# Where a state-space scan starts its exponentials: before or after it waits for the scan ahead of it

## The chip, the cores and the metric

One core of one Trainium2 chip runs the whole program. The metric is the device time of one execution in microseconds, taken as the median of several runs. Engines are named as in the profile: PE (TensorE), DVE (VectorE), ACT (ScalarE), POOL (GpSimd), SP (the queue that issues most transfers). Each engine works through its own list of instructions in the order in which they stand there, and waits where an operand isn't there yet.

## The reference, cut to what matters

The program is two layers of a small perceiver over 16 sequences of 64 tokens with 256 channels (1024 tokens): cross attention, attention and a tiled feed-forward layer, then a second cross attention, a state-space layer, and a mixture of 64 experts. The change is in the state-space layer. Its core is a recurrence over the 64 tokens of a sequence, for 8 heads of 64 states:

```python
dt = jax.nn.softplus(dt_proj + dt_bias)
dA = jnp.exp(A[None, None] * dt[..., None])
dB = B_proj * dt[..., None]
def step(h, inp):
    dA_t, dB_t, C_t, x_t = inp
    h = dA_t[..., None] * h + dB_t[..., None] * x_t[:, :, None, :]
    y_t = jnp.einsum('bns,bnsd->bnd', C_t, h)
    return (h, y_t)
...
y_heads = y_heads + D[None, None, :, None] * x_heads
y = y_heads.reshape(B, L, d) * jax.nn.silu(z)
return y @ W_out.T
```

Its result is added to x, normalised, and routed to 8 of 64 experts for each token.

## The kernel before, in words

The 1024 tokens are 8 groups of 128 (two sequences each), g = 0 to 7. The recurrence isn't run step by step. For every pair of tokens of a sequence the decay between them is the exponential of A times a sum of dt over the tokens between. The pairs are split into 6 levels (NL), by the highest bit in which the two places differ; at each level the sum splits at a midpoint into a part of the earlier token and a part of the later one. So for each group there are 6 tables of sums of dt and a seventh that holds dt itself.

*What feeds the scans.* `inlet(g)` (line 271 on) makes the convolved input `xtok` and the raw `dtr` of a group. `sums(lo, hi)` (line 314 on) makes softplus of it for four groups, one matmul pair `ps_seg` (L351) makes all sums, ACT copies them to `sg`, and a transfer writes them to DRAM as `segd` (L353). `sw["summed"]` tells how many groups have their sums. `sums(0, 4)` is finished before the scans start, `sums(4, 8)` runs beside the first of them.

*A scan.* `scan(g)` works in these steps; the names are those of the profile.
- Two transfers on SP's queue read the sums back from `segd`, spread over 64 partitions each, into `e` (L1329, 2 x 896 KB, two buffers). Four ACT operations turn them into exponentials in place (L1335).
- PE makes `ps_B` (L1340), DVE multiplies it by dt to `bt` (L1342); PE makes `ps_C` (L1347), ACT copies it to `cT` (L1349); PE makes the gate `ps_z` (L1353), ACT takes its tanh `zt` (L1361).
- For each level DVE makes `pb` from `bt` and `e` (L1365) and POOL makes `pc` from `cT` and `e` (L1366). DVE completes `zt` (L1369), POOL makes `pd` (L1371).
- Three rounds of two levels each: PE makes `ps_g` (L1380, 32 matmuls a round, each two records in the profile for every matmul of the source), and DVE writes it into the 128 x 128 matrix `gt` by masked copies (L1390, four a round). After the first round `sw["half"]` is set to g + 1.
- The diagonal: `ps_dg` (L1401), `dg` (L1403, DVE), `yt` (L1405, POOL). Then `ps_y` = `gt` times `xtok` (L1410), two DVE operations `yt` (L1411, L1412), PE's transposes `ps_yT` (L1416), ACT's copy `yT` (L1418), the output product `ps_o` (L1423), and DVE's addition to x (L1424).
- `route(g)` follows: a layer norm (DVE, with `rs_mo` by POOL at L205 and its result `xtok` at L216), transposes `psx_mo` (L1183), logits (L1188), some forty small DVE operations that pick the experts, places `ps_pos` (L1236), and the slots `idx` (L1248). For each token eight POOL scatters `xbuf` (L1158) send its row to its experts' slots; `post(n)` issues them four at a time inside later scans. `shared()` does the shared expert beside it (`ps_se` L1439, `hT_s` L1443 and L1444, `ps_sy` L1448).

*The order.* `drive` (line 235 on) is a small planner that runs while the program is built. Each scan is a generator that issues some instructions and yields two numbers, a cost and a gap in assumed microseconds; `drive` takes whichever generator is due next. At most two scans are active; a scan that yields "tail" (after `ps_o`) no longer counts, and the next one starts. `until(test)` yields until the test holds. Below `drive`, the framework may still interleave neighbouring pieces on an engine. All of it is fixed when the program is built: the chip sees one list for each engine.

In the code before, a scan's first step is this, and the next yield stands behind the exponentials:

```python
yield from until(lambda: sw["summed"] > g and sw["half"] >= g)
...
yield 0, 12.0
```

Every PSUM tile of the program comes from one pool of 8 buffers that are handed out in order.

Of the kernel before, what the change touches and what calls it, by code (L numbers as in the profile page):

```python
# [147 lines left out]
def perceiver_kernel(ctx: ExitStack, tc: tile.TileContext, a: dict, consts: bass.AP, out: bass.AP):  # L148
# [115 lines left out]
    sw = {"done": 0, "routed": 0, "half": 0}  # L264
    segd = dram.tile([NG * NH, (NL + 1) * P], F32, name="segd")

    def until(test):
        while not test():
            yield 0, 0.5
# [1006 lines left out]
    with p2:  # L1276
# [43 lines left out]
        def scan(g):  # L1320
            pb, gt = pbs[g % 2], gts[g % 2]
            tk = slice(g * P, (g + 1) * P)

            yield from until(lambda: sw["summed"] > g and sw["half"] >= g)

            e = wrk.tile([P, 4, NL + 1, P], F32, tag="e", name=f"e_{g}")
            src = segd.rearrange("(g j q) k -> g q j k", j=4, q=2)
            for q in range(2):
                nc.sync.dma_start(  # L1329
                    out=e[q * 64 : (q + 1) * 64, :, :, :].rearrange("p j l k -> p j (l k)"),  # L1330
                    in_=src[g, q].partition_broadcast(64),
                )
            dts = e[:, :, NL, :]
            for j in range(4):
                A.activation(e[:, j, 0:NL, :], e[:, j, 0:NL, :], AF.Exp, scale=Ac[:, j : j + 1])  # L1335
            yield 0, 12.0
            pm = psm([P, 4, P], f"ps_B_{g}")
            for j in range(4):
                for c in range(2):
# [115 lines left out]
        def wtile2(shape, name):  # L1455
# [3 lines left out]
            (2, [maker(inlet, g, wide("xn"), wtile2) for g in range(NG - 2, NG)]),  # L1459
            (1, [maker(sums, 4, NG)]),  # L1460
            (2, [maker(scan, g) for g in range(NG)]),
            (1, [outward, shared]),
        )
# [153 lines left out]
    with tc.If(n > CAP):  # L1617
        with tc.For_i(0, E) as e:
# [9 lines left out]
            for q in range(4):  # L1628
# [12 lines left out]
                for i in range(2):  # L1641
                    g = 2 * q + i
# [36 lines left out]
```

## Time and profile before

| | us |
|---|---|
| median of 3 runs | 1093.58 (1093.21 to 1094.02) |
| the profiled execution: its own time | 1105.71 |
| its span | 1103.9 |
| PE busy (share of the span) | 900.0 (82%) |
| DVE busy | 612.9 (56%) |
| ACT busy | 269.0 (24%) |
| POOL busy | 274.3 (25%) |
| transfers of `e` issued, first and last | 608.3 and 780.3 |
| first `ps_B` to last `ps_o` | 619.4 to 855.6 |
| last scatter to the experts' slots issued | 886.4 |

The scans take the stretch from 608 to 856 us of the span; before it lie both cross attentions and layer 0, after it the experts. Times below are microseconds from the start of the span of the profiled execution, which as a whole took 12 us more than the median of the runs. The clock of PE that the profile lists is a share of full speed; over the whole execution it was 0.878.

### The profile page before, as it was taken

How to read it: one execution, taken by the hardware profiler on the slowest of the kernel's cores; microseconds unless marked ns; L12 is line 12 of the kernel's file. 1: busy time of each engine (PE TensorE's matmuls, PEld its weight loads, DVE VectorE, ACT ScalarE, POOL GpSimd, SP SyncE). 2: the span in 40 equal slices, each digit the busy share in tenths (PEclk: the TensorE clock that was granted, in tenths of full speed). 3: DMA queues.
4: the chain of work that ended last, by engine and by line, in shares of the span. 5: the costliest groups of instructions: out<-in, count | busy, mean ns of one | idle time of the engine just before them, and what ended most of it. 6: DMA issues, size and time to landing. Idle time of an engine off the chain costs nothing. (4 is left out here: it accounts for less than half of the span.)

```text
span 1103.9 us, 16706 instructions
## 1 busy us (share of the span) xinstructions
PE 900.0 (82%) x6242; PEld 685.4 (62%) x6242; DVE 612.9 (56%) x1903; ACT 269.0 (24%) x608; POOL 274.3 (25%) x326
## 2 busy tenths in 40 slices
PE   4978888978898888978885788889988369999945
PEld 3755565655665565655644567778877258778724
DVE  1446564556546654555557747657866863333316
ACT  0314132222224132222224422113210022232210
POOL 0000100001100100000102112555565525556540
PEclk7879999999999999999887757677786579999978
DMA  7511150310420150111301632444411958888236
GB/s 235 172 38 61 61 180 1 121 61 28 154 108 14 62 180 1 60 62 44 111 2 37 153 72 68 108 108 98 108 47 41 351 184 286 280 291 287 72 121 265
DMA packets 70712, 130.60 MB, mean 118 GB/s; under 512 B 10083, under 2 KB 56607, under 8 KB 67558
## 3 DMA queue, kind: packets, MB, share of 16 engines
q1 hardware_dynamic: 56016, 107.97, 30.3%
q0 software_dynamic: 7680, 17.33, 4.5%
q10 hardware_dynamic: 6934, 4.23, 1.4%
q8 instruction: 50, 0.82, 0.3%
q14 instruction: 32, 0.26, 0.1%
HBM read 97.54 MB, written 36.14 MB: 121 GB/s over the span
## 5 line engine op out<-in xcount | busy, mean ns | idle before, releaser
L1524 POOL DMA_INDIRECT ybuf<-yo,goal x96 | 93.5, 974 | 87.3 <-DVE yo L1551 28.8
L1516 PE MATMUL ps_ee<-xT,wq 128*128 128x192 f32 x512 | 95.4, 330 | 0.2 <-ACT xT L1506 0.2
L1516 PEld LDWEIGHTS ps_ee<-xT,wq 128*128 128x128 f32 x512 | 81.8, 190 | 6.7 <-issue 3.5
L1158 POOL DMA_INDIRECT xbuf<-xtok,idx x64 | 68.1, 1064 | 66.4 <-DVE idx L1248 41.1
L989 PE MATMUL fpy<-fw,fxm 128*128 128x256 f32 x256 | 59.3, 391 | 13.3 <-DVE fxm L986 6.8
L625 PE MATMUL po_a<-cn,paT_a 128*64 128x256 f32 (+1 forms) x416 | 54.3, 395 | 15.7 <-ACT paT_a L619 7.7
L989 PEld LDWEIGHTS fpy<-fw,fxm 128*128 128x128 f32 x256 | 49.5, 196 | 23.9 <-issue 16.0
L1380 PEld LDWEIGHTS ps_g<-pc,pb 64*128 64x128 f32 x768 | 56.9, 228 | 10.5 <-POOL pc L1366 4.9
L1380 PE MATMUL ps_g<-pc,pb 64*128 64x64 f32 x768 | 59.8, 316 | 2.7 <-DVE zt L1369 1.6
L625 PE MATMUL po_b<-cn,paT_b 128*64 128x256 f32 (+1 forms) x416 | 50.2, 385 | 9.2 <-DVE paT_b L619 8.3
L205 POOL TENSOR_TENSOR rs_ff<-ve_ff,neghalf 128x1 f32<-128x1 f32 x8 | 4.4, 548 | 204.8 <-DVE ve_ff L203 193.3
L399 PE MATMUL psc<-ct,cn 128*128 128x128 f32 x384 | 51.9, 287 | 2.6 <-DMA cn<-in_ctx_dram 2.5
L1390 DVE COPY_PREDICATED gt<-ct,ps_g 128x256 f32<-128x256 uint32 x96 | 43.2, 538 | 12.3 <-PE ps_g L1380 7.3
L399 PEld LDWEIGHTS psc<-ct,cn 128*128 128x128 f32 x384 | 46.5, 149 | 5.5 <-issue 3.3
L587 PE MATMUL sc_b<-cT,qT_b 128*64 128x512 f32 (+1 forms) x256 | 47.5, 525 | 2.1 <-DVE qT_b L559 1.6
L1366 POOL TENSOR_TENSOR pc<-cT,e 128x256 f32<-128x256 f32 x48 | 36.3, 790 | 46.6 <-ACT cT L1349 46.5
L625 PEld LDWEIGHTS po_a<-cn,paT_a 128*64 128x64 f32 (+1 forms) x416 | 27.3, 139 | 32.4 <-ACT paT_a L619 8.7
L1518 ACT ACTIVATE hg<-ps_ee 128x192 f32<-128x192 f32 x64 | 21.4, 334 | 106.6 <-PE ps_ee L1516 39.2
L1504 PE MATMUL ps_xT<-ct,xg 128*128 128x128 f32 x192 | 30.5, 287 | 19.5 <-DMA xg<-xbuf 19.5
L587 PE MATMUL sc_a<-cT,qT_a 128*64 128x512 f32 (+1 forms) x256 | 46.4, 505 | 0.0
L194 ACT COPY cT<-psc 128x512 f32<-128x512 f32 x51 | 29.8, 588 | 66.8 <-PE psc L399 66.2
L625 PEld LDWEIGHTS po_b<-cn,paT_b 128*64 128x64 f32 (+1 forms) x416 | 27.8, 136 | 25.3 <-DVE paT_b L619 10.0
(438 smaller groups left out, 1858.2 us busy)
## 6 DMA issues: line engine op xcount, KB each, us to landing
cn<-in_ctx_dram SPq DMA_DIRECT2D x16, 1536.0 KB
e<-segd SPq DMA_DIRECT2D x16, 896.0 KB
xbuf<-zero SPq DMA_DIRECT2D x8, 1632.0 KB
xg<-xbuf SPq DMA_DIRECT2D x16, 816.0 KB
wq<-in_L_ffn_We_gate_dram SPq DMA_DIRECT2D x16, 512.0 KB
wq<-in_L_ffn_We_up_dram SPq DMA_DIRECT2D x16, 512.0 KB
wq<-in_L_ffn_We_down_dram SPq DMA_DIRECT2D x16, 512.0 KB
yg<-ybuf SPq DMA_DIRECT2D x8, 1024.0 KB
```

Source lines behind the costliest of these rows:

```text
L194: A.copy(dst, src)
L399: T.transpose(ps[:, j, :], cn[:, 4 * q + j, c * P : (c + 1) * P], ident)
L587: T.matmul(sc[b * 64 : (b + 1) * 64, :], lhsT=qT[:, c, b * 64 : (b + 1) * 64], rhs=cTs[2 * g + b][:, c, 512 * j : 512 * j + n], start=c == ...
L625: T.matmul(pos[j > 0][b * 64 : (b + 1) * 64, :], lhsT=paTs[j][:, i, b * 64 : (b + 1) * 64], rhs=cns[2 * g + b][0:r, k, :], start=k in (0, ...
L989: T.matmul(py, lhsT=xm[:, t, c, :], rhs=fw[:, 2 * h + t, c, :], start=h + t + c == 0, stop=h == 3 and t == 1 and c == 1,)
L1158: sct = G.indirect_dma_start(out=xbuf, out_offset=bass.IndirectOffsetOnAxis(ap=idx[:, g, k : k + 1], axis=0), in_=xtok[:, g, 0:DX], in_off ...
L1366: G.tensor_tensor(pc[:, l, :, :].rearrange("p j (k h) -> p j k h", h=1 << l), half(cT, l, 1), half(ev, l, 1), ALU.mult)
L1380: T.matmul(pgs[q][:, i, j, :], lhsT=pb[q * 64 : (q + 1) * 64, l + i, j, :], rhs=pc[q * 64 : (q + 1) * 64, l + i, j, :], start=True, stop=True,
L1390: V.copy_predicated(gt.rearrange("p (j q) (k u h) -> p q j k u h", q=2, u=2, h=h)[:, q, :, :, 1, :], _bc(lvl[:, l + i, :].rearrange("p (k ...
L1504: T.transpose(to, xgs[q][:, 2 * part + s, c * P : (c + 1) * P], ident)
L1516: T.matmul(pe[:, j, :], lhsT=w, rhs=xTs[q][:, i, c, :], start=c == 0, stop=c == 1)
L1524: arr = G.indirect_dma_start(out=ybuf, out_offset=bass.IndirectOffsetOnAxis(ap=goal, axis=0), in_=y, in_offset=None, bounds_check=NTOK * T ...
```

## The change

The wait at the start of a scan is split. A scan now waits only for its sums, issues the two transfers of `e`, lets 6 assumed microseconds pass, issues the four exponentials, lets 4 pass, and only then waits for the scan ahead to have issued its first round of `ps_g`. The gap of 12 that stood between the exponentials and `ps_B` is gone.

```diff
         def scan(g):
             pb, gt = pbs[g % 2], gts[g % 2]
             tk = slice(g * P, (g + 1) * P)
-
-            yield from until(lambda: sw["summed"] > g and sw["half"] >= g)
+            yield from until(lambda: sw["summed"] > g)
 
             e = wrk.tile([P, 4, NL + 1, P], F32, tag="e", name=f"e_{g}")
             src = segd.rearrange("(g j q) k -> g q j k", j=4, q=2)
...
                     in_=src[g, q].partition_broadcast(64),
                 )
+            yield 0, 6.0
             dts = e[:, :, NL, :]
             for j in range(4):
                 A.activation(e[:, j, 0:NL, :], e[:, j, 0:NL, :], AF.Exp, scale=Ac[:, j : j + 1])
-            yield 0, 12.0
+            yield 0, 4.0
+
+            yield from until(lambda: sw["half"] >= g)
             pm = psm([P, 4, P], f"ps_B_{g}")
```

No instruction is added or removed. What the split does to the lists, as the program is built, from the first scan on (a number behind a name is its group):

- PE, before: g0, g0, g0 (its three rounds), dg0, y0, yT0, o0, B1, C1, z1, g1, g1, g1, dg1, y1, yT1, o1, B2, and so on. From scan 3 on `ps_B` of a scan stands beside `ps_y` of the one ahead.
- PE, now: g0, g0, B1, g0, C1, dg0, z1, y0, g1, yT0, g1, o0, g1, dg1, y1 (with `psx_mo0` inside it), logit0, yT1, o1, B2, C2, z2, `psx_mo1`, logit1, g2, B3, g2, pos0, g2, C3, dg2, z3, y2, g3, pos1, yT2, g3, o2, g3, se0, dg3, sy0, y3, `psx_mo2`, logit2, yT3, o3, B4, C4, z4. Scans 0 and 1 are interleaved, and so are scans 2 and 3. From scan 4 on the list is nearly what it was (B6 now ahead of y5, z6 ahead of o5).
- POOL, before: pd2, 8 scatters, yt2, 2 scatters, pc3, pd3, 2 scatters, rs_mo2, 4 scatters, yt3, pc4. Now: pd2, two levels of pc3, 1 scatter, yt2, 3 scatters, the other four levels of pc3, pd3, 9 scatters, rs_mo2, 3 scatters, yt3, rs_mo3, pc4. Later: yt4, 7 scatters, pc5, pd5, rs_mo4, 8 scatters, yt5, pc6 (before: 2 scatters, yt4, 6 scatters, pc5, pd5, rs_mo4, 2 scatters, yt5, 6 scatters, pc6).
- ACT: the exponentials of scan 4 now stand ahead of the copy yT2, half of scan 5's ahead of yT3, the first of scan 3's ahead of yT1.
- SP: the same transfers of `e` in the same order, with nothing between them.

## The prediction

> **What bounds the kernel now.** I read the page's 40 slices first, then the busy times by stretch, then PE's timeline of one hand-over between scans, and last the queues of ACT, POOL and SP there.
>
> ```profile
> span 1103.9 us, 16706 instructions
> ...
> PE   4978888978898888978885788889988369999945
> ...
> PEclk7879999999999999999887757677786579999978
> ```
>
> The scans are slices 22 to 31. PE is busy in eight or nine tenths of them, but at 0.5 to 0.8 of its clock, the lowest of the program. By stretch (PE, PEld, DVE, ACT, POOL busy with counts, then clock, DMA share, GB/s):
>
> ```profile
> 638.00:685.70 47.70, 42.10 (x279) 35.02 (x280) 26.06 (x80) 14.02 (x20) 8.76 (x10) 0.64 0.35 79
> 685.70:751.30 65.60, 57.60 (x405) 51.90 (x403) 41.61 (x140) 12.11 (x20) 33.93 (x38) 0.72 0.34 91
> 751.30:776.50 25.20, 24.75 (x188) 22.26 (x188) 18.99 (x71) 6.00 (x10) 15.29 (x16) 0.80 0.52 118
> 776.50:803.50 27.00, 24.87 (x182) 22.38 (x180) 22.54 (x76) 5.88 (x11) 15.50 (x17) 0.75 0.43 105
> 803.50:832.00 28.50, 24.93 (x187) 22.20 (x188) 19.27 (x74) 2.74 (x7) 16.91 (x20) 0.82 0.14 46
> ```
>
> They run from ps_seg to the end of o1, from there to the end of z4, then from z to z of scans 5, 6 and 7. PE sets the pace, slowed by waits for short DVE, ACT and POOL steps, and by a clock that falls with them. The first stretch has the lowest clock; there scan 1 starts only after scan 0:
>
> ```profile
> 648.53 1.87 PE L1401 MATMUL ps_dg<-ct,pd 128*128 128x2 f32 x8
> 650.26 3.65 PE L1410 MATMUL ps_y<-xtok,gt 128*128 128x64 f32 x16
> 655.51 1.09 PE L1416 MATMUL ps_yT<-ct,yt 128*128 128x128 f32 x4 [1.60 <-DVE yt L1412]
> 657.28 3.73 PE L1423 MATMUL ps_o<-woT,yT 128*128 128x256 f32 x8 [0.68 <-ACT yT L1418]
> 660.84 1.95 PE L1340 MATMUL ps_B<-xnTm,winT 128*128 128x128 f32 x16
> ```
>
> Nothing of scan 1 stands between dg0 and o0. The clock in that time (columns as above):
>
> ```profile
> 644.20:647.60 3.40, 3.40 (x36) 3.40 (x34) 1.42 (x4) 1.20 (x2) 0.00 (x0) 0.50 0.81 166
> 647.60:651.00 3.40, 3.40 (x22) 3.28 (x20) 1.60 (x5) 0.00 (x0) 0.32 (x1) 0.50 0.00 0
> 657.80:661.20 3.40, 3.40 (x12) 2.72 (x11) 0.16 (x1) 2.73 (x4) 0.00 (x0) 0.56 0.00 0
> 661.20:664.60 3.40, 3.40 (x32) 3.40 (x31) 2.53 (x8) 0.00 (x0) 0.55 (x1) 1.00 0.00 0
> ```
>
> Full windows of ps_g, dg and y stay at 0.50; one window of o0, with 256-wide operands, brings 1.00. What e and its exponentials wait for:
>
> ```profile
> 670.20 1.24 SPq L1329 DMA_DIRECT2D e<-segd  x2
> ...
> 708.31 1.76 ACT L1335 ACTIVATE e<-e,Ac 128x768 f32<-128x768 f32 x2 [13.09 <-DMA e<-segd]
> ...
> 728.36 1.26 POOL L1371 TENSOR_TENSOR pd<-cT,bt 128x512 f32<-128x512 f32 x1
> ```
>
> The transfers go out at 636.29, 670.20, 696.10, 728.42, each when POOL has finished the pc of two scans earlier (e has two buffers): no list order can bring those forward by itself. e4 went out at 696.10, and ACT began on it at 708.31: 12.2 us.
>
> **The change part by part.** No instruction is added; what counts is order. Durations of one piece at full and at half clock, from PE's timeline: B or C 1.95 and 3.20; z 1.88 (at half clock twice that, an estimate); a round of g 2.00 and 3.55 (64 records in 7.09); dg 1.05 and 1.87; y 2.2 and 3.7; yT 0.6 and 1.1; o 1.89 and 3.73.
>
> *Scans 0 and 1.* Up to 641.5 nothing moves. Then, at half clock: second g0 to 645.1, B1 648.3, third g0 651.9, C1 655.1, dg0 656.9. z1 is dense and I let the clock rise in it: 659.0. y0 661.2; g1 663.2 (pc1 starts after yt0 on POOL, about 658, and has its first two levels by 659.5); yT0 664; g1 666; o0 668; g1 670; dg1 671. Now DVE is in front: x, st, mv, ve and xtok of group 0 with POOL's rs_mo (0.42 + 0.43 + 0.18 + 0.15 + 0.55 + 0.53 = 2.3 us after o0) stand ahead of the last four masked copies of gt1 (4 x 0.43), so y1 begins at about 672.2 and with psx_mo0 ends at 675; two yt (0.69 each, with a sig of 0.2) 676.7; yT1, copy 0.58, o1 at either clock: 680 to 682, against 685.7. If B1's window already raises the clock (742.8 to 746.2, mostly B4, did so), every piece from 647 on is short and o1 ends near 676; if z1 doesn't raise it, 683. I take 680: **-6 us**, ends -10 and -3.
>
> *Exponentials ahead of other ACT work.* e3's first now stands ahead of yT1's copy. Its transfer goes out when pc1 ends, about 663, lands 12.2 later at 675; yT1 wants ACT at 677. e4's four (3.41 us) stand ahead of yT2: counted from the end of o1, pc2 ends at +10, lands +22, exponentials done +26, yT2 wanted at +27.5. They are hidden behind y; without these margins of 2 and 1.5 us, each us that a transfer is late is one on the yT copy, o and what follows. Cost taken: 0; ends 0 and +4.
>
> *Scans 2 and 3*, from the end of o1 (S). B2, C2, z2, psx_mo1, logit1 to S+8.7, then at full clock g2, B3, g2, pos0, g2 to S+17, C3 S+19, dg2, z3 S+22, y2 S+24. On DVE idx0 now comes after fit0 and all but one of gt0's copies: about S+22.4, against 694.4 in the trace (S+8.7). The scatters hang on idx0, so POOL's list runs from there: 1 scatter (1.28 from start to start), yt2 1.05, 3 scatters 3.9, four levels of pc3 3.0, pd3 1.27, 9 scatters 11.6, rs_mo2 0.6, 3 scatters 3.9, yt3 1.05 = 27.7, so yt3 is there at S+50. Queued behind rs_mo2: DVE's xtok of group 2 (S+46), behind that dg3 and hT_s0, behind these PE's sy0, behind it y3 (S+48 to S+52). Then yt3, yT3, the copy, o3, B4, C4, z4: 11 to 14 us more, z4 at S+61 to S+66. The trace has 65.6. Taken: **-1**, ends -5 and +4 (clock and DVE delays that the list doesn't show).
>
> *Scans 4 to 7.* PE's list is nearly the same, the stretches measure 25.2, 27.0 and 28.5. A gain: POOL's idle of 8.46 us ahead of scan 5's scatters, which wait for idx3, goes, as idx3 stands earlier. A loss: yt5 stands behind six more scatters (7.7 us), covered by B6 and C6 for 4. Taken: 0, ends -4 and +4. From o7 on the lists are equal, so the shift reaches the end whole: the expert weights are requested at 855.6, when o7 ends.
>
> Sum: -6 + 0 - 1 + 0 = -7 us, on the profiled execution 1105.7 to 1098.7. It ran 12 us longer than the median; I take the 7 off the median: 1093.6 - 7 = **1086.6 us**.
>
> [...]
>
> **The rivals.** *One: hand-over gained, then given back (same time).* What scan 1 gains, scans 2 and 3 lose at POOL. For it: the transfers follow pc, so from scan 2 on the change asks for nothing sooner. Against: +4 is the end of my bound there. -6 + 4 + 2 = 0: 1093.6.
>
> *Two: the clock stays up.* B, C and z now stand between the rounds of g in scans 1 and 3, and dense windows raise the clock. At 1.00 the PE time of the first two stretches would shrink by 42.10 x 0.36 + 57.60 x 0.28 = 31 us; half of it would meet DVE and POOL: -16, 1077.6. Against: g, dg and y windows, which keep it at 0.50, are still there, and POOL's list bounds scan 3.
>
> *Three, slower: POOL's late scatters.* Nine scatters ahead of rs_mo2, seven between yt4 and pc5, eight ahead of yt5. At the median they cost 1.28 us each; the slowest took 2.18. With DVE held up too: one msk operation (L1225) took 5.63 us, ending with POOL's pd at 780.84. [...] If each of the three queues loses 4 us, that is +12 against -6: +6, 1099.6. It decides from 6 us on, or idx0 coming at S+29 rather than S+22.
>
> *Four: it doesn't do what it says*, B1 held by something else (PSUM, DVE's bt1). bt1 stands after eight copies of gt0 whose inputs are there, and e1, sent out behind e0 at 608, has landed by 631, where the transfers' share falls to nothing. I give it no price of its own; it ends as rival one does.
>
> **How the numbers follow.** Forecast -3 to -11: 0.46. Rival one and four, within 2.2 us: 0.13. Two: 0.13. Three: 0.28. I count 0.2% (2.2 us) as what a measurement of this kernel tells from none. So faster 0.59, same 0.13, slower 0.28. The likeliest case's own range is 1082 to 1091; all good ends together would make -19, all bad ones +9, neither likely; to hold eight in ten I go to rival two's price and a little over, and to three's: 1076 to 1099.
>
> **What would show it.** B1 on PE near 645 and o1 before 683: step one right; o1 at 685 or later: wrong. z4 less than 66 us after o1: step two. rs_mo2 waited on by DVE for several us, and PE idle before sy0: POOL's queue as walked. The clock at 1.00 through 650 to 700: rival two. ACT waiting for e4 with yT2 queued: the margin was too small. The prediction fails if scans 4 to 7, whose lists hardly change, move by more than 4 us.

## The result, and the profile after

| | median, us | runs |
|---|---|---|
| changed kernel | 1087.39 | 16, from 1080.56 to 1096.92 |
| kernel before, on the same chip | 1096.84 | 16, from 1090.17 to 1104.38 |

The ratio is 0.9913, 95% interval 0.9891 to 0.9934: the changed kernel is 9.5 us faster. The profiled execution took 1092.37 us. Two repeats, told of below, gave 0.9974 (0.9944 to 1.0004) and 0.9954 (0.9926 to 0.9982). The three intervals don't all overlap; weighted by the inverse squares of their widths they give 0.994, or -6.6 us of 1097.

The page of the changed kernel, its span, PE and PE's granted clock by slices:

```profile
span 1090.6 us, 16700 instructions
...
PE   4978888978899788988786689979888449999955
...
PEclk7889999999999999999888767978786569999978
```

The clock in slices 22 to 31, the scans, now reads 8, 7, 6, 7, 9, 7, 8, 7, 8, 6; before it read 7, 7, 5, 7, 6, 7, 7, 7, 8, 6. Busy time by stretch, with the same cuts in each kernel: from the second ps_seg to the end of o1, to the end of z4, z5, z6, z7, and to the end of o7. Columns: length, busy PE, PEld, DVE, ACT and POOL with counts, then PE's clock, DMA share and GB/s. The changed kernel:

```profile
640.53:686.33 45.80, 42.60 (x279) 35.24 (x280) 23.31 (x68) 13.97 (x20) 8.33 (x10) 0.65 0.35 80
686.33:749.67 63.34, 53.80 (x402) 45.45 (x401) 47.34 (x162) 12.26 (x20) 32.34 (x36) 0.81 0.36 94
749.67:771.71 22.04, 20.84 (x193) 18.47 (x193) 18.89 (x72) 5.94 (x10) 13.44 (x16) 1.00 0.56 125
771.71:797.00 25.29, 21.64 (x171) 19.78 (x171) 13.04 (x40) 4.04 (x7) 18.66 (x22) 0.73 0.49 126
797.00:823.85 26.85, 24.39 (x199) 21.21 (x197) 24.99 (x98) 4.40 (x8) 13.64 (x14) 0.87 0.12 38
823.85:849.20 25.35, 21.70 (x145) 19.86 (x144) 17.46 (x60) 1.78 (x4) 15.27 (x18) 0.56 0.14 45
sum 208.67, PE 184.97 PEld 160.01 DVE 145.03 ACT 42.39 POOL 101.68; mean PE 30.83 PEld 26.67 DVE 24.17 ACT 7.06 POOL 16.95
```

The last stretch and the sum for the kernel before (its first stretch with this cut is 47.32 long, 42.13 busy):

```profile
831.95:855.56 23.61, 20.46 (x148) 18.27 (x148) 15.18 (x61) 1.78 (x4) 13.12 (x15) 0.64 0.13 42
sum 217.15, PE 194.66 PEld 171.98 DVE 143.23 ACT 42.52 POOL 103.47; mean PE 32.44 PEld 28.66 DVE 23.87 ACT 7.09 POOL 17.24
```

The scans became 217.15 - 208.67 = 8.5 us shorter with the same number of PE records (1382). PE's busy time fell by 9.7, and its idle time rose from 22.5 to 23.7. So PE waits no less than before; it does the same work at a higher clock (0.76 over the six stretches, 0.72 before). In the stretch from z4 to z5 the clock is 1.00 where it was 0.80. The first stretch, where I put 6 of my 7 us, gave 1.5. These two profiles are of different kinds (see the last section), so the 8.5 us need not be the change's alone; two profiles from one chip, shown below, have 7.0 us less busy time too, but 7.1 more of idle time.

The time behind o7, where the lists are equal, was 248.3 us before and 241.4 after. That is no effect of the change, as the repeats will show; it is why the two profiled executions differ by 13.3 us and the medians by 9.5.

### The profile page after: what moved, and what is told of

It is laid out like the page before. It is cut to its first block, busy times and chain, and to the rows that moved or that the text cites. A ratio compares the mean times of both kernels' runs of the same rounds, so it can differ in the third digit from the quotient of the medians.

```text
span 1090.6 us, 16700 instructions
## 1 busy us (share of the span) xinstructions
PE 891.7 (82%) x6242; PEld 674.3 (62%) x6242; DVE 614.7 (56%) x1903; ACT 272.4 (25%) x608; POOL 272.3 (25%) x326
## 5 line engine op out<-in xcount | busy, mean ns | idle before, releaser
L1158 POOL DMA_INDIRECT xbuf<-xtok,idx x64 | 64.8, 1012 | 43.1 <-issue 15.2
L989 PE MATMUL fpy<-fw,fxm 128*128 128x256 f32 x256 | 62.4, 406 | 13.3 <-DVE fxm L986 6.8
L625 PE MATMUL po_a<-cn,paT_a 128*64 128x256 f32 (+1 forms) x416 | 55.5, 402 | 15.7 <-ACT paT_a L619 7.7
L399 PE MATMUL psc<-ct,cn 128*128 128x128 f32 x384 | 49.6, 280 | 2.7 <-DMA cn<-in_ctx_dram 1.6
L587 PE MATMUL sc_b<-cT,qT_b 128*64 128x512 f32 (+1 forms) x256 | 47.3, 524 | 2.1 <-DVE qT_b L559 1.6
L625 PEld LDWEIGHTS po_b<-cn,paT_b 128*64 128x64 f32 (+1 forms) x416 | 27.7, 136 | 25.4 <-DVE paT_b L619 10.0
```

What stands on the lines that cost most here:

```text
L399: T.transpose(ps[:, j, :], cn[:, 4 * q + j, c * P : (c + 1) * P], ident)
L587: T.matmul(sc[b * 64 : (b + 1) * 64, :], lhsT=qT[:, c, b * 64 : (b + 1) * 64], rhs=cTs[2 * g + b][:, c, 512 * j : 512 * j + n], start=c == ...
L625: T.matmul(pos[j > 0][b * 64 : (b + 1) * 64, :], lhsT=paTs[j][:, i, b * 64 : (b + 1) * 64], rhs=cns[2 * g + b][0:r, k, :], start=k in (0, ...
L989: T.matmul(py, lhsT=xm[:, t, c, :], rhs=fw[:, 2 * h + t, c, :], start=h + t + c == 0, stop=h == 3 and t == 1 and c == 1,)
L1158: sct = G.indirect_dma_start(out=xbuf, out_offset=bass.IndirectOffsetOnAxis(ap=idx[:, g, k : k + 1], axis=0), in_=xtok[:, g, 0:DX], in_off ...
```

## The experiments

Three theories stood at first: (1) the hand-over from scan 0 to scan 1 brings the gain, (2) it comes piece by piece and most of it behind z4, (3) the stretches of single traces are chance.

**Scan 1 alone, scans 1 to 3, scans 4 to 7** (all three on one chip, where the median of the kernel before was 1100.3). Each applies the change to some scans:

```diff
-            yield from until(lambda: sw["summed"] > g)
+            early = g == 1          # 1 <= g <= 3;  g >= 4
+            yield from until(lambda: sw["summed"] > g and (early or sw["half"] >= g))
...
-            yield 0, 6.0
+            if early:
+                yield 0, 6.0
...
-            yield 0, 4.0
+            yield 0, 4.0 if early else 12.0
```

> The change for scan 1 alone: scan 1 asks and takes its exponentials early and its gap is short; the other scans keep the old wait and the old gap of 12. PE's list is the changed kernel's up to the end of o1 and from scan 2 on that of the kernel before, but for a place or two. Theory 1 (the prediction's first step: the gain is the hand-over from scan 0 to scan 1): -6 us against the kernel before. Theory 2 (what the two traces show by stretch: -1.5 to the end of o1, the rest later): -1.5. Theory 3 (the trace's stretches are chance, any order gives about the same): 0 within 3.

> The change for scans 1 to 3 alone, scans 4 to 7 with the old wait and gap. Theory 1: nearly all of the gain, -7. Theory 2: -1.5 and -2.3 for the first two stretches, about -4; the stretches of scans 5 to 7 stay at 25 to 28 us. Theory 3: 0 within 3.

> The change for scans 4 to 7 alone, scans 1 to 3 with the old wait and gap. Theory 1 (scans 4 to 7 are bound by the same lists): 0. Theory 2 (about -5 of the gain comes there, by the two traces): -5, with the stretch from z4 to z5 near 22 us. Theory 3: 0 within 3.

| scans changed | ratio, 95% | us | ps_seg to end of o1 | ps_seg to end of o7 | PE busy | PE idle |
|---|---|---|---|---|---|---|
| 1 | 0.9965 (0.9937 to 0.9993) | -3.9 | 39.1 | 202.6 | 182.7 | 20.0 |
| 1 to 3 | 0.9978 (0.9954 to 1.0003) | -2.4 | 45.9 | 217.0 | 182.1 | 34.9 |
| 4 to 7 | 0.9961 (0.9938 to 0.9984) | -4.3 | 47.4 | 208.3 | 189.5 | 18.8 |

Theory 1 falls with the second and third row: scans 1 to 3 bring less than half of 7 (their median, 1100.63, is no lower than that of the kernel before), and scans 4 to 7, for which it had 0, bring 4.3. Theory 2 fits all three within the intervals. They don't rule out theory 3, since each reaches within 3 us of the kernel before. One expectation of the second row failed: its stretches of scans 5 to 7 were to stay at 25 to 28 us, and took 22.7, 35.5 and 22.9.

The first row's profile was of its fastest execution (1081.53; the median is 1096.37). It shows the same list up to o1 as the changed kernel, done in 39.1 instead of 45.8 us. The traces show where they part. In all 14, each stretch in which the clock stays at 0.50 or at 1.00 lasts a whole multiple of 3.41 us, but for the last, which ends with the profile (from 639.17 on in the changed kernel's: 23.89, 13.65, 10.24, 27.31). Here are two neighbouring windows of 3.41 us, cut along the clock's stretches, in the first row's profile; B1 begins in the first of them (columns as above):

```profile
641.88:645.29 3.41, 3.41 (x22) 3.29 (x21) 1.43 (x4) 1.45 (x2) 0.00 (x0) 0.50 0.90 181
645.29:648.70 3.41, 3.41 (x46) 3.22 (x45) 2.40 (x7) 0.00 (x0) 0.00 (x0) 1.00 0.02 6
```

Behind the window with B1 the clock is up, 9 us behind ps_seg. In the changed kernel's profile B1, g, C1 and z1 all run at 0.50, and the clock rises 22.5 us behind ps_seg, where z1 ends:

```profile
646.00:649.41 3.41, 3.41 (x24) 3.29 (x23) 1.42 (x4) 1.51 (x2) 0.00 (x0) 0.50 0.88 179
649.41:652.82 3.41, 3.41 (x26) 3.19 (x26) 1.67 (x4) 0.00 (x0) 0.00 (x0) 0.50 0.02 5
...
659.64:663.05 3.41, 3.41 (x5) 1.54 (x6) 0.50 (x2) 0.00 (x0) 2.94 (x4) 0.50 0.00 0
663.05:666.46 3.41, 3.41 (x43) 3.23 (x43) 1.99 (x3) 2.24 (x3) 3.41 (x5) 1.00 0.00 0
```

B1's own busy time in the window in which it begins, first row and changed kernel (only the columns of PE, PEld and DVE, then clock, DMA share and GB/s):

```profile
641.88:645.29 3.41, 2.24 (x10) 2.24 (x11) 0.00 (x0) 0.50 0.90 181
646.00:649.41 3.41, 2.18 (x10) 2.18 (x11) 0.00 (x0) 0.50 0.88 179
```

Six other profiles with this list up to o1, but for the place of psx_mo0 in one (the changed kernel's three, scans 1 to 3, and two told of below), took 45.8 to 46.3; in them B1 fills 2.01 to 2.18 us of its first window. So the early rise is the rarer case, one profile of seven, and in that one B1 fills the most of its first window.

The second row shows what rival three feared, though behind z4. Its lists put seven scatters between pd5 and rs_mo4. The timeline of POOL there:

```profile
782.02 1.01 POOL L1158 DMA_INDIRECT xbuf<-xtok,idx  x1 [0.16 <-issue]
...
789.70 0.97 POOL L1158 DMA_INDIRECT xbuf<-xtok,idx  x1 [0.31 <-issue]
790.69 0.58 POOL L205 TENSOR_TENSOR rs_mo<-ve_mo,neghalf 128x1 f32<-128x1 f32 x1
```

That of DVE, same kernel:

```profile
779.01 0.15 DVE L203 TENSOR_SCALAR ve_mo<-mv_mo 128x1 f32<-128x1 f32 x1
791.31 0.58 DVE L216 TENSOR_SCALAR xtok<-x,mv_mo,rs_mo 128x256 f32<-128x256 f32 x1 [12.14 <-POOL rs_mo L205]
```

And that of PE:

```profile
791.94 0.69 PE L1183 MATMUL psx_mo<-ct,xtok 128*128 128x128 f32 x2 [9.19 <-DVE xtok L216]
```

The input of rs_mo was there at 779.2; POOL came to it at 790.7; DVE stood for 12.14 us and PE for 9.19.

**Is asking early worth anything?** One kernel keeps the early request and puts the gap back behind the second wait; the other is the kernel before without its gap.

```diff
             yield from until(lambda: sw["half"] >= g)
+            yield 0, 12.0 if g else 2.0
```

> Transfer and exponentials early as in the changed kernel, but the old gap of 12 put back behind the wait for the other scan (for scan 0, 2, so that it has its old 12 in all). On PE each scan then begins after the one ahead of it, nearly as before; on ACT the exponentials stand early. If asking early is worth something by itself (the change's words): half of the gain or more, -4 to -9. If only the missing gap, which lets a scan's B, C, z and first rounds of g stand inside the scan ahead, brings the gain (theories 1 and 2): 0, from -2 to +3.

```diff
-            yield 0, 12.0
+            yield 0, 12.0 if g == 0 else 0.0
```

> The kernel before with one number changed: the gap between the exponentials and ps_B is 0 (for scan 0 it stays 12); transfers and exponentials are asked for as late as before. PE's list then rolls: B, C and z of each scan stand inside the one ahead, not only in scans 1, 3 and 5. If the gap was what held the time and asking early is worth nothing by itself: at or below the changed kernel, -8 to -14 against before. If asking early is what matters: the late exponentials stand straight ahead of the products that need them, DVE's bt and all behind it wait some 10 us for each transfer, +10 or more. The clock in the scans should be higher than before's 0.64 to 0.82 if dense B, C and z between the rounds of g raise it.

Early with the gap: 1.029 (1.0258 to 1.0323), +32 us, which neither side had expected. Late without the gap, on another chip (median of the kernel before 1109.9): 0.9928 (0.9884 to 0.9972), -8.0 us, within its interval as good as the change. PE is busy 185.3 us in the scans and idle 23.0; the two profiles of the kernel before, which are of the same kind as this one, have 194.7 and 22.5, 194.3 and 21.5. So the gap mattered, its gain is busy time of PE, and no run shows that the early request brings anything. The transfers show why: in the changed kernel e3, e4 and e5 go out at 665.65, 695.77 and 715.45, in the kernel without the gap at 668.18, 688.73 and 705.95, each within 0.1 us of the end of POOL's pc of two scans earlier, which frees the buffer. The first of these, changed kernel:

```profile
661.23 4.39 POOL L1368 TENSOR_TENSOR pc<-cT,e 128x256 f32<-128x256 f32 x6
```

The +32 has two parts: PE's busy time is 206.2 us at a clock of 0.69 (each scan's B, C and z stand behind the scan ahead again), and its idle time 41.1: on POOL the pc of scans 2, 3, 5 and 7 now stands right behind six to eight scatters, and PE waits 4.01, 3.41 and 3.38 for three of them.

**The clock, with B, C and z as one piece**, for scan 1, then for all scans from 1 on (both, and the next experiment, on the chip of the kernel without the gap).

```diff
             V.tensor_tensor(bt, pm, dts, ALU.mult)
-            yield 1.8, 0
+            if g != 1:              # g == 0
+                yield 1.8, 0
...
             A.copy(cT, pm)
-            yield 1.8, 0
+            if g != 1:
+                yield 1.8, 0
...
-            yield 1.7, 1.0
+            yield (1.7 if g != 1 else 5.3), 1.0
```

> The changed kernel with B, C and z of scan 1 issued as one piece. PE has them in one dense stretch behind the second round of g0; the rounds of g1 come earlier, and scans 0 and 1 are closely interleaved. Theory C (the clock decides the first stretch: the same list took 45.8 us where the clock rose at 663 and 39.1 where B1's window raised it): the dense stretch raises the clock about 650 in every execution, ps_seg to the end of o1 is 38 to 41 us, and the median lies 3 to 6 us below the changed kernel's, -12 to -15 against before. Theory O (order and the waits on DVE and POOL decide): within 2 us of the changed kernel, with o1 waiting for gt1 or yt1.

> The changed kernel with B, C and z of every scan but the first issued as one piece: scans pair off, 0 with 1, 2 with 3, 4 with 5, 6 with 7. Theory C: each pair has one dense stretch that raises the clock, granted clock in the scans 0.8 to 0.9, -15 against before. Theory O: the pairs give their work to DVE and POOL at once (12 levels of pc, 2 of yt and 16 scatters), PE waits more, and between pairs nothing covers o, route and the next B: 0 to +10.

The first: 0.9958 (0.9925 to 0.9992), -4.7 us against before, where theory C had -12 to -15. With the dense piece the clock is up early (at 656.87, 12 us behind ps_seg; 22.5 in the changed kernel's first profile), and the first stretch is, with the 36.6 of the second kernel, the shortest of all:

```profile
644.68:681.30 36.62, 34.35 (x274) 28.89 (x274) 18.42 (x45) 12.49 (x17) 8.71 (x10) 0.79 0.44 100
```

Yet most of the 9.2 us won there is gone at the end of y3, which comes 95.1 us after ps_seg; in the changed kernel it comes after 94.9 in the first profile and after 98.3 in the second, which is of this one's kind. POOL stands idle 11.42 us until idx0 lets the scatters start at 705.26, and PE waits 3.18 for pc3 and 7.17 for gt3. (DVE copies gt3 behind xtok, which stands 7.21 us, until POOL has made rs_mo2 behind twelve scatters.) So theory C was right on the clock and wrong on the total; that idx0 and POOL's list behind it hold scan 3 wherever scan 1 ends fits these waits, but was not tested by itself. For all scans: 1.0189 (1.0147 to 1.0231), 230.0 us for the scans, 37.9 of them idle, at a clock of 0.71. Theory O had the sign, and +10 at most; measured +21. The longest of the waits is 7.75 us for yt2, with DVE and POOL serving two scans at once.

**Taking the root off POOL.** This computes 1/sqrt in the route's layer norm in another way.

```diff
-        G.tensor_tensor(rs, ve, neghalf[:, 0:1], ALU.pow)
+        if name.startswith("mo"):
+            V.tensor_scalar(rs.bitcast(I32), ve.bitcast(I32), -0.5, 1597463007.0, ALU.mult, ALU.add)
+            for i in range(3):
+                t = small.tile([P, 1], F32, tag="ln_t", name=f"t_{name}_{i}")
+                V.tensor_tensor(t, rs, rs, ALU.mult)
+                V.scalar_tensor_tensor(t, t, -0.5, ve, ALU.mult, ALU.mult)
+                V.scalar_tensor_tensor(rs, t, 1.5, rs, ALU.add, ALU.mult)
+        else:
+            G.tensor_tensor(rs, ve, neghalf[:, 0:1], ALU.pow)
```

> The changed kernel with the reciprocal root of the route's layer norm made on DVE (a guess by bits and three Newton steps, ten small operations of about 0.16 us) instead of by POOL, for the eight groups of the scans. rs_mo2 no longer stands behind nine scatters. If POOL's late scatters cost what the trace shows (PE idle 4.84 us before ps_sy, rival three's place): that wait goes, and the median falls 2 to 5 us below the changed kernel's, -11 to -14 against before. If that wait is only the place where PE would wait anyhow (yt3, behind the same scatters): -1 to +2 against the changed kernel, since DVE gets 1.6 us more for each group.

1.0218 (1.0175 to 1.0261), +24 us: both expectations miss. The ten operations are not 1.6 us in a row. DVE's list puts copies of gt, pieces of pb and small operations of the route between them, and five of the ten of group 1 took 0.68 to 0.82 us each, all while POOL made pc (695.35 to 700.80). For that group the chain from ve to xtok took from 692.4 to 701.1, and PE waited 4.90 for it. And the wait before ps_sy of scan 3 did not go, it grew to 9.78, though rs_mo2 needed nothing from POOL. DVE there:

```profile
735.86 0.16 DVE L209 TENSOR_TENSOR t_mo<-rs_mo 128x1 f32<-128x1 f32 x1
741.68 0.43 DVE L1400 COPY_PREDICATED gt<-ct,ps_g 128x256 f32<-128x256 uint32 x1 [5.67 <-remote]
743.79 1.10 DVE L1400 COPY_PREDICATED gt<-ct,ps_g 128x256 f32<-128x256 uint32 x3 [1.68 <-remote]
744.79 0.15 DVE L210 SCALAR_TENSOR_TENSOR t_mo<-t_mo,ve_mo 128x1 f32<-128x1 f32 x1
```

The copies of gt3 wait for PE's third round, whose records end at 736.73; they begin 5 us later, in the middle of twelve scatters that POOL issues in a row (730.30 to 745.37). "Remote" means that the profile can't name what ended the wait. The experiment left rival three's price open and found a second hold at the same place.

**The same two kernels again, and the change without scans 2 and 3** (on another chip, where the median of the kernel before was 1107.27).

```diff
-            early = g == 1
+            early = g == 1 or g >= 4
```

(against the kernel with scan 1 alone)

> The kernel before, unchanged, for a second profile on the chip that also runs the changed kernel beside it, so that stretches are compared on one chip. If the first two profiles were alike in all but the change: ps_seg to the end of o1 47 us, o1 to z4 66, z4 to the end of o7 104, end of o7 to the end of the span 248. If they came under different conditions: the time behind o7, which the change does not touch, is here the same as in the changed kernel's profile beside it (241 or 248 in both).

> The changed kernel, unchanged, for a second profile and more times. Theory C (which window raises the clock decides the first stretch, and it may fall out either way in any execution): ps_seg to the end of o1 is near 46 (clock up at z1 or y0, some 20 us behind ps_seg) or near 39 (clock up in B1's window, within 10 us of ps_seg), nothing between, and the stretches behind o1 repeat within 2 us: 63 to z4, 99.5 from z4 to the end of o7. Median 0.989 to 0.993 of the kernel before.

> The change for scan 1 and for scans 4 to 7; scans 2 and 3 with the old wait and the old gap of 12, so that they are not interleaved and POOL's nine scatters do not stand ahead of rs_mo2. If the parts add up (scan 1 alone 0.9965, scans 4 to 7 alone 0.9961 of the kernel before) and the change gains nothing in scans 2 and 3: 0.992 to 0.993, the same as the changed kernel within 2 us. If interleaving scans 2 and 3 brings its 2 us: 2 us above the changed kernel. If it costs (rival three): 3 to 6 us below it.

The changed kernel, unchanged: 0.9974 (0.9944 to 1.0004); without scans 2 and 3: 0.9942 (0.9915 to 0.9970). The first stretch came as theory C has it (45.8), but the ratio and the stretches behind o1 did not repeat: 66.7 us to z4 where 63 was expected, 103.4 from there to the end of o7 where 99.5 was. The sums over the six stretches on this chip, kernel before:

```profile
sum 215.79, PE 194.32 PEld 171.48 DVE 142.02 ACT 42.40 POOL 103.60; mean PE 32.39 PEld 28.58 DVE 23.67 ACT 7.07 POOL 17.27
```

and changed kernel:

```profile
sum 215.91, PE 187.28 PEld 161.14 DVE 145.80 ACT 42.38 POOL 101.75; mean PE 31.21 PEld 26.86 DVE 24.30 ACT 7.06 POOL 16.96
```

PE is busy 7.0 us less again, and idle 7.1 us more (21.5 to 28.6): all of it given back. Behind o7 both have 246 to 248 us, so that part is not the change's. Where the idle time went is seen at scan 3. PE's timeline, changed kernel, this chip:

```profile
735.51 2.08 PE L1450 MATMUL ps_sy<-wsh,hT_s 128*128 128x256 f32 x4 [8.23 <-DVE hT_s L1446]
```

DVE's, where it copies gt3:

```profile
728.76 1.43 DVE L1392 COPY_PREDICATED gt<-ct,ps_g 128x256 f32<-128x256 uint32 x4 [5.27 <-PE ps_dg L1403]
730.76 0.59 DVE L216 TENSOR_SCALAR xtok<-x,mv_mo,rs_mo 128x256 f32<-128x256 f32 x1 [0.56 <-issue]
734.51 0.17 DVE L1405 TENSOR_TENSOR dg<-ps_dg,Db 128x8 f32<-128x8 f32 x1 [3.17 <-remote]
```

The same place in the changed kernel's first profile, PE:

```profile
730.08 2.08 PE L1450 MATMUL ps_sy<-wsh,hT_s 128*128 128x256 f32 x4 [4.84 <-DVE hT_s L1446]
```

and DVE:

```profile
722.56 1.43 DVE L1392 COPY_PREDICATED gt<-ct,ps_g 128x256 f32<-128x256 uint32 x4 [1.13 <-PE ps_g L1382]
...
728.68 0.59 DVE L216 TENSOR_SCALAR xtok<-x,mv_mo,rs_mo 128x256 f32<-128x256 f32 x1 [4.69 <-POOL rs_mo L205]
```

In the first profile rs_mo2, behind its nine scatters, holds DVE. Here the copies are held for longer, as in the kernel with the root on DVE, so that xtok behind them hardly waits for rs_mo2 any more (0.56), and dg, whose input PE finished by 727.3, is held once more (3.17).

The kernel with scans 2 and 3 left alone has none of these waits. Its profile, which was of its fastest execution (1090.38; the median is 1099.95), shows no wait of PE between ps_seg and the end of o7 over 2 us, and the least idle time of all profiles, 15.7, beside 185.5 busy; the scans take 201.2 us. Its median is 4.4 us under the changed kernel's on this chip, inside the 3 to 6 expected if interleaving scans 2 and 3 costs; but the two intervals overlap, so that it beats the change is likely and not shown.

**A third time** (again another chip, where the median of the kernel before was 1098.32).

> The changed kernel, unchanged, a third time. Two ratios stand: 0.9913 (beside a median of 1096.8 for the kernel before; the profile then had 241 us behind o7) and 0.9974 (beside 1107.3; 247 us behind o7, PE 8.2 us idle ahead of ps_sy of scan 3 instead of 4.8). Theory K (the two go together: under the conditions with the slower median the nine scatters ahead of rs_mo2 hold DVE's copies of gt3 up, and the gain of scans 4 to 7 goes too): a median of the kernel before near 1100 or less goes with 241 us behind o7, less than 5 us ahead of ps_sy and 0.989 to 0.993; one near 1107 or more with 247, more than 7 us and 0.995 to 1.000. Theory N (chance between runs): about 0.994 whichever it is.

0.9954 (0.9926 to 0.9982). The trace repeats the first one stretch by stretch (46.0, 63.1, 22.0, 25.4, 26.8 and 25.8 us; PE waits 4.86 before ps_sy; 240.3 us behind o7). So theory K holds for the waits, but its ratio was to be under 0.993; the ratio is nearer theory N's 0.994.

## Why the prediction was right, and where it was not

**The total, right.** -7 forecast; -9.5 measured, -6.6 over the three comparisons. Two terms of the sum were mis-sized, in opposite directions: that they cancel is luck.

**Scans 0 and 1, mis-sized.** The list did what the step says: PE's idle time in the first stretch fell from 5.2 to 3.2 us, scan 1 runs inside scan 0. But "z1 is dense and I let the clock rise in it" was the choice that made -6, and it failed: B1 and C1 took 3.78, z1 3.63, o1 again 3.78 at half clock, and o1 ended at 686.33, not 680. Measured -1.5, outside my own ends of -10 and -3. (I had 3.20 as the price of B at half clock, read from the B at 685.52, in which the clock rises at 688.13; at half clock throughout it is 3.78, which is most of the way from -3 to -1.5.) My own test said "o1 at 685 or later: wrong". (The scans began 2.1 us later in the span; set against the second g0 the stretch is still 1.5 shorter only.) The end of -10, "if B1's window already raises the clock", is what the kernel with scan 1 alone shows: 47.3 - 39.1 = -8.2. Which of the two comes is not in the list: B1 began 1.17 us into its window of 3.41 us there and 1.24 to 1.41 us in the six others.

**Exponentials ahead of other ACT work: 0, right.** e4's began at 707.73 after 0.77 us of waiting, and the copy yT2 (712.58) waited for PE alone.

**Scans 2 and 3: -1, about right, by two larger terms.** The walk held: nine scatters, rs_mo2 at 728.04, DVE and ps_sy held behind it. It was covered by what I had left to rival two: with B3, C3 and z3 between the rounds of g the clock is at 1.00 from 686.96 to 714.26 in the changed kernel (before, it was at 0.50 from 698.37 to 718.85), and PE's busy time fell from 57.63 to 53.80. (That this order is needed for it is not shown: the kernel with scans 2 and 3 left alone is busy 185.5 us in the scans, the changed kernel 185.0 and 187.3.) Net -2.3 in the first pair; +1.1 in the second comparison, where the hold of the copies and of dg came in its place and was longer.

**Scans 4 to 7: 0, mis-sized.** 104.2 became 99.5 us in the first pair, and this exceeds the 4 us at which I said the prediction fails. "PE's list is nearly the same" was wrong in what mattered: B4, C4 and z4 now stand together behind o3 instead of beside y3, and behind them, from z4 to z5, PE runs at 1.00 (0.80 before). All three profiles of the changed kernel show it, 22.0 us each; both of the kernel before have 25.1. It does not hang on the early start of scans 4 to 7: with scans 1 to 3 alone B4, C4 and z4 stand together there as well (22.7 us at 1.00), and with scans 4 to 7 alone y3 and yT3 stand between them (23.0 at 1.00). The loss walked for POOL's pc5 came too, as 1.10 us of waiting before g5. In the second comparison the gain was lost again behind z7 (28.8 us to the end of o7 against 24.2).

**Rivals.** Two is the nearest to what the traces show, at 9.7 us of busy time rather than 16, though its sign did not come: through 650 to 700 the clock was at 0.50 up to 663.06 and again from 676.72 to 686.96. Three was real where scatters stand ahead of a small POOL operation (PE waited 4.84 and 9.19), but paid by two's gain; the 8.23 of the second comparison came from the other hold. One is what the profiles of the second comparison show: 215.8 against 215.9 for the scans as a whole. Four is out: B1 began at 647.2, right behind the second round of g0.

**Left open:** why the copies of gt3 start late on two of the chips, and with it how much of the gain stays on such a chip: of the 7.0 us of busy time in the second comparison the scans kept none.

## What to carry to other kernels

Split a stretch's gain into busy and idle time of the engine that bounds it: here a change meant to remove waits left PE's waits as long (23.7 us in the scans, 22.5 before) and went with a higher clock (0.76, 0.72 before). On a list that runs half its time at half clock (99 of 209 us in the changed kernel's scans), look at where B, C, z and o stand (the next section has the counts); but packed together by hand, as tried here, B, C and z went with a clock of 0.79 rather than 0.65 in the first stretch and brought no more than the change (0.9958 of the kernel before for one scan, 1.0189 for all). And asking for a transfer earlier in the program brought nothing here, where e3, e4 and e5 went out within 0.1 us of the end of the pc that frees their buffer; look first at what the issue waits for.

## What was not expected of the hardware

- The same instructions up to o1 took 39.1 us in one profile and 45.8 to 46.3 in six. The clock rose 9 us behind ps_seg in the one and 22.5 in the changed kernel's first profile; PE's busy time was 36.15 and 42.60 us, its idle time 2.9 and 3.2.
- In full windows the clock stayed at 0.50 or went up with no difference in PE's busy share (3.41 of 3.41 in both). Cut into windows of 3.41 us along their clock records, the scans of the 14 traces hold 440 at half clock. Of the 276 with less than 1.5 us of B, C, z, o, se and sy (all with operands of 128 elements and more) none was followed by 1.00, though PE was busy throughout 151 of them with g, dg, y and the like; of the 53 with 3 us or more all were; in between it went either way (the first profiles of the two kernels have 42 of the former and 8 of the latter). These are counts; what makes the clock rise is not shown.
- Profiles fall into two kinds. Behind o7 six have 240.3 to 242.3 us, and eight have 246.1 to 249.3; all runs that shared a chip are of one kind, the first profile of the kernel before is of the second, the first of the changed kernel of the first. Only profiles of the second kind show copies of gt held for several us beside POOL's scatters (5.67 and 5.27 above). They also hold fewer records: 7154 to 7432 semaphore events (from which the profile infers what ended a wait), against 9388 to 9404 in the six others. Whether the longer times come from the chip or from the recording is not shown. Two traces are to be compared only when they are of one kind, best from one chip.
